# Turning rows with VectorE and small transfers instead of TensorE, and storing expert slots from GpSimd

## The chip, the cores and the metric

The kernel runs on one core of a Trainium2 chip. A core has five engines, each with its own in-order stream of instructions: TensorE (PE in the profile; its weight loads are PEld), VectorE (DVE), ScalarE (ACT), GpSimd (POOL) and SyncE (SP, which only starts transfers here). They meet through semaphores. The metric is the device time of one execution in microseconds (us); lower is better.

## What is computed

The reference is a stack of four layers on x (4 batches, 256 tokens, 256 features), float32 throughout. Each layer adds a cross attention to a context (4 x 512 x 128) and then a feed-forward, both on layer-normalised rows:

```
x = x + L0_xattn(layernorm(x), ctx)   # 16 heads of 16, normalised queries and keys, 16 extra context rows
x = x + L0_ffn(layernorm(x))          # best 4 of 64 "arrows" per token, low rank, plus a dense product
x = x + L1_xattn(layernorm(x), ctx)   # 16 heads of 128, 8 key/value heads
x = x + L1_ffn(layernorm(x))          # softmax router, best 2 of 8 experts, SwiGLU, plus a shared expert
x = x + L2_xattn(layernorm(x), ctx)   # as L1
x = x + L2_ffn(layernorm(x))          # each token to one of two experts
x = x + L3_xattn(layernorm(x), ctx)   # as L1
x = x + L3_ffn(layernorm(x))          # best 64 tokens of a batch through a wide feed-forward
```

## The kernel before

**Turned rows.** A matrix product contracts over partitions, so the rows that enter it must be stored with features on partitions. A batch's normalised rows xn lie with tokens on partitions, as [128, 2 halves, 256]; `layernorm_T` (L938 to L948) turns them into xnT by four TensorE transposes against an identity matrix into a PSUM bank, which ScalarE copies to SBUF. `context_T` (L906 to L911) does the same for a batch's context, four transposes and one copy, into cT. `turned1` (L2189 to L2196) stores the rows of layer 1's feed-forward to the DRAM buffer xd, from which tokens are later gathered by index, and turns them as well for the router.

**Order.** The large stages stand in a block in which the program's order is the order of TensorE, ScalarE, VectorE and GpSimd. SyncE is not in that list; the framework places its transfers itself.

**Layer 0's attention** walks through the batches b in eight half-steps i. `between(b, i)` (L1589 on) prepares batch n = b + 1: for n of 2 and 3, half-step 0 turned the context, copied its last rows (`last_context`, on GpSimd) and turned the normalised rows.

**Attentions 1 to 3** (`attention`, from L1795) walk through 32 units: a batch b and a pair of heads hp, 0 to 7. A unit makes the next unit's queries on TensorE (`queries`: seven block products and then sums on VectorE and ScalarE, `four`), then scores (L1923), exponentials on ScalarE (L1926) and the product with the context (L1931). GpSimd and VectorE add up the exponentials (`summed`) and divide. Beside this the next batch's rows are readied: in pair 1 the statistics (`Norm`), in pair 3 the normalised tokens, in pair 5 `layernorm_T`, in pair 6 `x_sums`, which adds blocks of the turned rows on VectorE for the seven-product scheme. The first batch of each attention is turned ahead of it. The callback `beside1` (L2248) does the router's work for batch b - 1 during attention 1: `Norm` in pair 3, tokens in pair 4, `turned1` in pair 5, `chosen` in pair 6, each at the end of its unit. Weights of the next feed-forward come on SyncE in batch 0, each behind the end of a unit (`load_waiting`).

**Layer 1's feed-forward** packs the chosen tokens into 20 slots (blocks) of 128. The loop over j (L2567 on) keeps several blocks going at once. Iteration j gathers block j+2 (`gather`, an indirect DMA by GpSimd, four buffers), transposes it on TensorE (`turn_in`), multiplies block j+1 with its expert's weights (`rise`), and block j with the second matrices (`fall`). At every odd j the pair (j-1, j) is finished by `last_rows` and `store`: ScalarE scales PSUM into yr, and a transfer on SyncE writes yr to the DRAM buffer yd. In the code, gather(j+2) and turn_in(j+2) stand first in an iteration, the stores last:

```
for j in range(-1, NBLK + 1):
    if j + 2 < NBLK:
        if j + 2 >= 4:
            blocks[j + 2].gather()
        ...
        blocks[j + 2].turn_in()
    ...
            for one in pair:
                one.store()
```

When all slots are stored, indirect DMAs by GpSimd (`Back`, L2505 on) fetch each token's two results from yd.

Of the kernel before, what the change touches and what calls it, by code (L numbers as in the profile page):

```python
# [9 lines left out]
F32 = mybir.dt.float32  # L10
# [7 lines left out]
P = 128  # L18
B, S, D = 4, 256, 256
NC = S // P  # L20
ND = D // P
# [815 lines left out]
def bounded_path(ctx: ExitStack, tc: tile.TileContext, t, out: bass.AP, over):  # L837
# [8 lines left out]
    first = ctx.enter_context(ExitStack())  # L846
    f0w = first.enter_context(tc.tile_pool(name="f0w", bufs=1, side="right"))
    w0 = first.enter_context(tc.tile_pool(name="w0", bufs=2, side="right"))
    ring = first.enter_context(ExitStack())
    ringo = ctx.enter_context(ExitStack())  # L850
    banks = {
# [99 lines left out]
        xn = Norm(b, name).tokens(keep)  # L951
        return xn, layernorm_T(xn, name)

    def normalised(name):

        after = layernorm(0, f"{name}_0")
        for b in range(B):
            _, xnT = after
            if b + 1 < B:
                after = layernorm(b + 1, f"{name}_{b + 1}")  # L960
            yield b, xnT

    raws = {}

# [68 lines left out]
    with tc.manual_schedule(engines={E.PE, E.Activation, E.DVE, E.Pool}):  # L1033
# [555 lines left out]
        def between(b, i):  # L1589

            n = b + 1
            if n == 1:
                if i == 0:
                    for k0 in range(0, NK, 2):
                        project_k(n, k0)()
                    scale[n] = Scale(n)
                    scale[n].square(False, NC, NQK)
                    xnTs[n] = layernorm_T(xns[n], f"a0_{n}")
                elif i == 1:
                    project_q(n)()  # L1600
                    scale[n].square(False, 0, NC)
                    project_v(n)
                elif i == 2:
                    scale[n].sum()
                    scale[n].power()
                elif i == 5:
                    transposed(n, 0)
                    transposed(n, 2)
                elif i == 6:
                    transposed(n, 4)  # L1610
            elif n < B:
                if i == 0:
                    context_T(n)
                    last_context(n)
                    xnTs[n] = layernorm_T(xns[n], f"a0_{n}")
                elif i == 1:
                    project_q(n)()
                elif i == 2:
                    for k0 in range(0, NK, 2):
                        project_k(n, k0)()  # L1620
                    scale[n] = Scale(n)
                    scale[n].square(False)
                elif i == 3:
                    project_v(n)
                    scale[n].sum()
                elif i == 4:
                    scale[n].power()
                elif i == 6:
                    transposed(n, 0)
                    transposed(n, 2)  # L1630
            if n + 1 < B:
                if i == (5 if n == 1 else 6):
                    norms[n + 1] = Norm(n + 1, f"a0_{n + 1}")
                elif i == (6 if n == 1 else 7):
                    xns[n + 1] = norms[n + 1].tokens()

            i0 = 4 if b == B - 1 else 6
            if b > 0 and i in (i0, i0 + 1):
                output0(b - 1, (i - i0,))
            if b == 1:  # L1640
                if i == 0:
                    bias_rows()
                elif i == 1:
                    bias_columns()
                elif i == 2:
                    output_bias()
            if b == B - 1:
                if i == 0:

                    mf = w0.tile([B * NK, P], F32, tag="hs", name="mf", bufs=1)  # L1650
                    nc.vector.tensor_copy(mf, m8)
                    xns["mf"] = mf
                elif i == 1:
                    pmk = bank("mm", [P, B * NK], "pmk")
                    nc.tensor.transpose(pmk, xns["mf"], ident[: B * NK, : B * NK])
                    nc.vector.tensor_scalar(
                        mbias.rearrange("p b k -> p (b k)"), pmk, 1.0, -NEG, ALU.subtract, ALU.mult
                    )
                elif i == 2:
                    score_bound()  # L1660
                elif i == 3:

                    nc.vector.tensor_reduce(
                        quad[:, :32], ident.rearrange("p (a q) -> p q a", q=32), AX.X, ALU.add
                    )
                    for j in range(1, 4):
                        nc.vector.tensor_copy(quad[:, 32 * j : 32 * (j + 1)], quad[:, :32])
            if b == B - 1:
                if i in (0, 2, 6):
                    norms["f", i // 2] = Norm(min(i // 2, 2), f"f0_{min(i // 2, 2)}")  # L1670
                if i in (1, 3, 7):
                    xns["f", i // 2] = norms["f", i // 2].tokens()
                if i in (3, 5):
                    k = (i - 3) // 2
                    xnTs["f", k] = layernorm_T(xns["f", k], f"f0_{k}")
                if i == 4:
                    arrows[0] = Arrows(0)
                    arrows[0].vectors()
                if i == 5:
                    arrows[0].routes()  # L1680
# [114 lines left out]
    def attention(L, m_sb, n_sb, first_xnT=None, after=None, at_end=None, chunk=None, within=None):  # L1795
# [11 lines left out]


        with tc.tile_pool(name=f"att{L}", bufs=2) as ap:
            xnTs, xns, xxs, norms, qTs, pqs, outs, sums = {}, {}, {}, {}, {}, {}, {}, {}  # L1810
            units = [(b, hp) for b in range(B) for hp in range(H // 2)]
            m_x = ap.tile([P, H // 2, 3, P], F32, tag="m_x", name=f"m_x{L}", bufs=1)
            n_x = ap.tile([P, H // 2, 3, P], F32, tag="n_x", name=f"n_x{L}", bufs=1)
# [220 lines left out]
            for n, (b, hp) in enumerate(units):  # L2034
                if b + 1 < B:
                    if hp == 1:
                        norms[b + 1] = Norm(b + 1, f"a{L}_{b + 1}")
                    elif hp == 3:
                        xns[b + 1] = norms[b + 1].tokens()
                if n == 0:  # L2040
                    first_queries(1)
                    x_sums(0)
                elif n + 1 < len(units):
                    queries(*units[n + 1])
                if b + 1 < B and hp == 5:
                    xnTs[b + 1] = layernorm_T(xns[b + 1], f"a{L}_{b + 1}")
                if b + 1 < B and hp == 6:
                    x_sums(b + 1)
                if b == 0:
                    m_sums((hp + 2) % (H // 2))  # L2050
                if n:
                    summed(*units[n - 1], *half)

                last, i = ((b, 0), hp - 4) if hp >= 4 else ((b - 1, 1), hp)
                prev = last[0] >= 0
                h0 = 4 * last[1]
                if prev and i >= 2:
                    for k in (2 * i - 4, 2 * i - 3):
                        o_sums(last[0], h0 + k, nc.gpsimd)
                half = heads(b, hp)  # L2060
                if prev and i == 0:
                    quotients(*last)
                if prev and i in (1, 2):
                    for k in (2 * i - 2, 2 * i - 1):
                        divided(last[0], h0 + k, nc.gpsimd)
                if b == 0 and hp < 6:
                    n_sums(hp)
                if (b, hp) == (1, 0):
                    n_sums(6)
                    n_sums(7)  # L2070
                if prev and i == 3:
                    out = Output(*last)
                    if last != (B - 1, 0):
                        out.products()
                        out.add()
                if after:
                    after(b, hp)
# [108 lines left out]
    nc.vector.memset(taken[:, 0, :], 0.0)  # L2186
    xnT1 = {}

    def turned1(b, xn):  # L2189
        nc.sync.dma_start(xd[b * S : (b + 1) * S, :].rearrange("(c p) d -> p c d", p=P), xn)  # L2190
        xnT1[b] = fx.tile([P, ND, S], F32, tag=f"xnT{b}", name=f"xnT_f1_{b}")
        pt = bank("t", [P, ND, S], f"pxn_f1_{b}")
        for c in range(NC):
            for d in range(ND):
                nc.tensor.transpose(pt[:, d, c * P : (c + 1) * P], xn[:, c, d * P : (d + 1) * P], ident)
        nc.scalar.copy(xnT1[b], pt)  # L2196
# [51 lines left out]
    def beside1(b, hp):  # L2248
        if b == 0:
            load_waiting(2)  # L2250
        if b > 0:
            if hp == 3:
                ahead1[b] = Norm(b - 1, f"f1_{b - 1}")
            elif hp == 4:
                ahead1[b] = ahead1[b].tokens()
            elif hp == 5:
                turned1(b - 1, ahead1[b])
            elif hp == 6:
                chosen(b - 1)

# [4 lines left out]
    with tc.manual_schedule(engines={E.PE, E.Activation, E.DVE, E.Pool}):  # L2265
        back = ExitStack()
        backp = back.enter_context(tc.tile_pool(name="back", bufs=4, side="right"))
        with tc.tile_pool(name="f1", bufs=2) as fp:
# [161 lines left out]
            class Block:  # L2430
# [66 lines left out]
                def store(self):  # L2497
# [2 lines left out]
                    done["slots"] = nc.scalar.activation(  # L2500
                        yr, self.py, AF.Copy, scale=state["wslot"][:, j : j + 1]
                    ).ins
                    nc.sync.dma_start(yd[j * P : (j + 1) * P, :], yr)

            class Back:  # L2505

# [947 lines left out]
```

## Time and profile before

| | us |
|---|---|
| median of 3 runs | 1388.01 |
| the runs | 1386.84 to 1388.09 |
| the profiled execution | 1386.64 |
| its span, first to last instruction | 1384.9 |
| TensorE busy | 1374.5 |
| VectorE busy | 887.1 |
| GpSimd busy | 683.9 |
| ScalarE busy | 580.2 |

The mean granted TensorE clock is 0.999 of full speed. A row of a timeline gives the start in us from the span's start, the busy time, the engine, the line of the code, the operation and its tiles; in brackets, the idle time before it and what ended that. Matmuls overlap in TensorE's pipeline, so their busy columns add up to more than the time that passes; starts are what counts. A float32 matmul is listed as two instructions, a transpose as one. The rows that give a stretch's busy time have its start and end, its length, busy us of TensorE, weight loads, VectorE, ScalarE and GpSimd with their numbers of instructions, the granted clock, the share of DMA and GB/s.

Where the stages lie in this execution: attention 1 from 217 to 541 us or so, the slots of layer 1's feed-forward from 575 to 628, attention 2 from 650 to 970, attention 3 from 1028 to 1352.

### The profile page before, as it was taken

How to read it: one execution, taken by the hardware profiler on the slowest of the kernel's cores; microseconds unless marked ns; L12 is line 12 of the kernel's file. 1: busy time of each engine (PE TensorE's matmuls, PEld its weight loads, DVE VectorE, ACT ScalarE, POOL GpSimd, SP SyncE). 2: the span in 40 equal slices, each digit the busy share in tenths (PEclk: the TensorE clock that was granted, in tenths of full speed). 3: DMA queues.
4: the chain of work that ended last, by engine and by line, in shares of the span. 5: the costliest groups of instructions: out<-in, count | busy, mean ns of one | idle time of the engine just before them, and what ended most of it. 6: DMA issues, size and time to landing. Idle time of an engine off the chain costs nothing.

```text
span 1384.9 us, 20011 instructions
## 1 busy us (share of the span) xinstructions
PE 1374.5 (99%) x7277; PEld 908.1 (66%) x7277; DVE 887.1 (64%) x2026; ACT 580.2 (42%) x1148; POOL 683.9 (49%) x829
## 2 busy tenths in 40 slices
PE   9999999999999999999999999999999999999998
PEld 7665676566656667887565666666975656666667
DVE  6667863665666547655666756558656758566676
ACT  5766454433343332356434333333364344333331
POOL 4223333566565445232577654556315675445561
PEclk9999999999999999999999999999999999999999
DMA  5000220300000001172110000000332000000001
GB/s 170 2 1 2 76 77 21 78 17 1 9 0 9 1 9 34 47 238 67 39 54 8 16 1 9 0 0 16 120 117 65 8 4 4 0 1 0 1 0 34
DMA packets 50849, 47.10 MB, mean 34 GB/s; under 512 B 8755, under 2 KB 46868, under 8 KB 50742
## 3 DMA queue, kind: packets, MB, share of 16 engines
q1 hardware_dynamic: 46406, 37.69, 8.9%
q0 software_dynamic: 2544, 6.95, 1.8%
q8 instruction: 60, 0.98, 0.3%
q10 hardware_dynamic: 1792, 1.10, 0.3%
q14 instruction: 47, 0.39, 0.1%
HBM read 38.78 MB, written 6.95 MB: 33 GB/s over the span
## 4 chain that ended last, share of the span: by engine, by line
PE 95%; POOL 2%; DVE 1%; DMA 1%; issue 0%; ACT 0%; ACTq 0%; SPq 0%; POOLq 0%; DVEq 0%
PE ps L1923 23%; PE po L1931 23%; PE paq L1893 6%; PE pao L1893 5%; PE pbq L1893 4%; PE pbo L1893 4%; PE ps L1378 3%; PE po L1388 2%; PE pyf L1512 2%; PE paf L1462 2%; PE pgu L2471 2%; PE psh L2292 2%; PE py L2017 2%; PE pn L1008 1%; PE pb L2876 1%; PE pm L992 1%
## 5 line engine op out<-in xcount | busy, mean ns | idle before, releaser
L1942 POOL TENSOR_TENSOR half<-pT 128x1024 f32<-128x1024 f32 x93 | 218.4, 2349 | 287.1 <-ACT pT L1926 214.8
L1923 PE MATMUL ps<-qT,cT 128*128 128x512 f32 x768 | 345.6, 593 | 0.0
L1931 PE MATMUL po<-pT,c_sb 128*128 128x512 f32 x768 | 345.3, 592 | 0.0
L1926 ACT ACTIVATE pT<-ps,mbias 128x512 f32<-128x512 f32 x384 | 263.8, 687 | 155.3 <-PE ps L1923 140.0
L1931 PEld LDWEIGHTS po<-pT,c_sb 128*128 128x128 f32 x768 | 145.8, 190 | 183.2 <-issue 183.2
L1923 PEld LDWEIGHTS ps<-qT,cT 128*128 128x128 f32 x768 | 138.9, 190 | 138.4 <-issue 136.3
L1935 ACT COPY oT<-po 128x512 f32<-128x512 f32 x96 | 56.2, 586 | 265.2 <-PE po L1931 265.2
L1978 POOL TENSOR_TENSOR oT<-oT,wide 128x512 f32<-128x512 f32 x84 | 106.8, 1292 | 0.0
L1903 DVE TENSOR_TENSOR qT<-qT,paq 128x128 f32<-128x128 f32 x90 | 25.5, 283 | 96.0 <-ACT qT L1902 96.0
L1382 ACT ACTIVATE pT<-ps 128x512 f32<-128x512 f32 x128 | 66.0, 602 | 25.8 <-PE ps L1378 25.6
L1950 DVE TENSOR_TENSOR half<-half 128x512 f32<-128x512 f32 x96 | 71.8, 748 | 2.7 <-POOL half L1940 2.5
L1952 DVE STREAM_TRANSPOSE turned<-half 128x512 f32<-128x512 f32 x96 | 68.3, 711 | 6.3
L1903 DVE TENSOR_TENSOR w<-w,pao 128x128 f32<-128x128 f32 x21 | 6.0, 286 | 103.0 <-ACT w L1902 103.0
L1893 PE MATMUL paq<-xnT_a,m_sb 128*128 128x128 f32 x360 | 71.4, 280 | 0.0
L1893 PE MATMUL paq<-xx,m_x 128*128 128x128 f32 x360 | 69.6, 275 | 0.0
L1893 PEld LDWEIGHTS paq<-xnT_a,m_sb 128*128 128x128 f32 x360 | 57.2, 192 | 16.7 <-issue 8.5
L1956 DVE TENSOR_REDUCE sums<-turned 128x16 f32<-128x512 f32 x96 | 65.9, 686 | 3.3
L1893 PE MATMUL pao<-n_x,ox 128*128 128x128 f32 x336 | 65.0, 275 | 0.0
L1902 ACT COPY qT<-paq 128x128 f32<-128x128 f32 x90 | 23.9, 265 | 94.1 <-PE paq L1893 94.1
L1906 DVE TENSOR_TENSOR qT<-qT,pbq 128x384 f32<-128x384 f32 x90 | 49.9, 554 | 9.7 <-DVE qT L1905 0.5
L1893 PEld LDWEIGHTS paq<-xx,m_x 128*128 128x128 f32 x360 | 54.7, 192 | 0.0
L1977 DVE STREAM_TRANSPOSE wide<-rz 128x512 f32<-128x512 f32 x84 | 54.4, 686 | 0.0
(490 smaller groups left out, 2547.3 us busy)
## 6 DMA issues: line engine op xcount, KB each, us to landing
wq<-in_L_wqT SPq DMA_DIRECT2D x11, 512.0 KB, 4.2
wo<-in_L_wo SPq DMA_DIRECT2D x11, 512.0 KB, 5.1
yd<-yr SPq DMA_DIRECT2D x20, 128.0 KB, 3.6
xd<-xn_f SPq DMA_DIRECT2D x8, 256.0 KB, 2.3
w<-in_F_w SPq DMA_DIRECT2D x4, 512.0 KB, 3.3
wk<-in_L_wkT SPq DMA_DIRECT2D x11, 128.0 KB, 4.0
wv<-in_L_wvT SPq DMA_DIRECT2D x11, 128.0 KB, 4.4
yd<-yb SPq DMA_DIRECT2D x9, 128.0 KB, 2.4
```

What stands on the lines that cost most here:

```text
L1382: nc.scalar.activation(pT[kp][:, j], ps[j], AF.Exp)
L1893: nc.tensor.matmul(p[:, at, :], lhsT=lhsT, rhs=rhs, start=(k == 0 and at == 0), stop=(k == len(of) - 1 and i == which[-1]),)
L1923: nc.tensor.matmul(ps, lhsT=cT[:, b, k * P : (k + 1) * P], rhs=qT, start=True, stop=True)
L1926: nc.scalar.activation(pT[:, k, :], ps, AF.Exp, bias=mbias[:, b, k : k + 1])
L1931: nc.tensor.matmul(po, lhsT=c_sb[:, b, k, :], rhs=pT[:, k], start=(k == 0), stop=(k == NK - 1))
L1935: done["head"] = nc.scalar.copy(raw, po).ins
L1942: nc.gpsimd.tensor_tensor(half, pT[:, 0:2], pT[:, 2:4], ALU.add)
L1950: nc.vector.tensor_tensor(part, half[:, 0], half[:, 1], ALU.add)
L1952: nc.vector.transpose(turned.rearrange("p f i -> p (f i)"), part)
L1956: nc.vector.tensor_reduce(sums[b, hp // 4][:, hp % 4, :], turned, AX.X, ALU.add)
L1977: nc.vector.transpose(wide, rzs[b, hp // 4][:, hp % 4, :, None].to_broadcast([P, NB, 32]))
L1978: eng.tensor_tensor(outs[b, hp], outs[b, hp], wide.rearrange("p f i -> p (f i)"), ALU.mult)
```

## The change

Nine turns in attentions 1 to 3 (batches 1 to 3), three of layer 1's router rows (batches 0 to 2) and two contexts in layer 0 (batches 2 and 3) are no longer TensorE's. VectorE transposes their 32 x 32 squares into a buffer y, and 16 transfers on SyncE, of 32 partitions each in runs of 128 bytes, carry the squares to their partitions of xnT or cT. In attentions this starts in pair 3 with the tokens instead of pair 5; the router's starts at the end of pair 4 instead of 5; a context starts in half-step 2 of the batch before, so six half-steps ahead of its use. The buffer y is a new pool in layer 0, and otherwise takes turns with xn in a tag of two buffers. The slots' stores are started by GpSimd instead of SyncE, at the same place of the code.

```
+    early = first.enter_context(tc.tile_pool(name="early", bufs=1, side="right"))
...
+    def squares(shape, name, soon):
+        return early.tile(shape, F32, tag="y", name=name) if soon else lnp.tile(shape, F32, tag="xn", name=name)
+
+    def turned_aside(dst, src, name):
+
+        y = squares([P, 4, 4, 32], f"y_{name}", True)
+        nc.vector.transpose(
+            y.rearrange("p q n s -> p n q s"), src.rearrange("p (n q s) -> p n q s", q=4, s=32)
+        )
+        to = dst.rearrange("p (n i s) -> p i n s", i=4, s=32)
+        for i in range(4):
+            for q in range(4):
+                nc.sync.dma_start(to[32 * q : 32 * q + 32, i], y[32 * i : 32 * i + 32, q])
+
+    def layernorm_aside(xn, name, xnT, soon=False):
+
+        y = squares([P, 4, ND, NC, 32], f"y_{name}", soon)
+        for c in range(NC):
+            nc.vector.transpose(
+                y[:, :, :, c].rearrange("p q d s -> p d q s"), xn[:, c, :].rearrange("p (d q s) -> p d q s", d=ND, s=32)
+            )
+        to = xnT.rearrange("p d (c i s) -> p i d c s", c=NC, s=32)
+        for i in range(4):
+            for q in range(4):
+                nc.sync.dma_start(to[32 * q : 32 * q + 32, i], y[32 * i : 32 * i + 32, q])
+        return xnT
+
+    def rows_tile(name):
+        return lnp.tile([P, ND, S], F32, tag="xnT", name=f"xnT_{name}")
...
             elif n < B:
                 if i == 0:
-                    context_T(n)
                     last_context(n)
                     xnTs[n] = layernorm_T(xns[n], f"a0_{n}")
...
             if n + 1 < B:
+                if i == 2:
+                    turned_aside(cT[:, n + 1, :], c_sb[:, n + 1].rearrange("p k c -> p (k c)"), f"c{n + 1}")
...
                     elif hp == 3:
-                        xns[b + 1] = norms[b + 1].tokens()
+                        name = f"a{L}_{b + 1}"
+                        xnTs[b + 1] = layernorm_aside(norms[b + 1].tokens(), name, rows_tile(name))
...
-                if b + 1 < B and hp == 5:
-                    xnTs[b + 1] = layernorm_T(xns[b + 1], f"a{L}_{b + 1}")
...
-    def turned1(b, xn):
+    def turned1(b, xn, aside=False):
         nc.sync.dma_start(xd[b * S : (b + 1) * S, :].rearrange("(c p) d -> p c d", p=P), xn)
         xnT1[b] = fx.tile([P, ND, S], F32, tag=f"xnT{b}", name=f"xnT_f1_{b}")
+        if aside:
+            layernorm_aside(xn, f"f1_{b}", xnT1[b])
+            return
...
             elif hp == 4:
-                ahead1[b] = ahead1[b].tokens()
-            elif hp == 5:
-                turned1(b - 1, ahead1[b])
+                turned1(b - 1, ahead1[b].tokens(), True)
...
-                    nc.sync.dma_start(yd[j * P : (j + 1) * P, :], yr)
+                    nc.gpsimd.dma_start(yd[j * P : (j + 1) * P, :], yr)
```

An unused generator, normalised, goes as well.

More of the change, by code (lines that the diff above doesn't have):

```diff
@@ L952, in layernorm @@
         return xn, layernorm_T(xn, name)
[L954 to L961, printed above, removed]
+    def squares(shape, name, soon):
[22 more added lines that the diff above has]
+        return lnp.tile([P, ND, S], F32, tag="xnT", name=f"xnT_{name}")
     raws = {}
@@ L1809, in attention @@
         with tc.tile_pool(name=f"att{L}", bufs=2) as ap:
-            xnTs, xns, xxs, norms, qTs, pqs, outs, sums = {}, {}, {}, {}, {}, {}, {}, {}
+            xnTs, xxs, norms, qTs, pqs, outs, sums = {}, {}, {}, {}, {}, {}, {}
             units = [(b, hp) for b in range(B) for hp in range(H // 2)]
```

## The prediction, made before the changed kernel was run

> **What bounds the kernel now.** I read part 1 of the page first, the summary and the chain next, then the timeline of the stage in which the slots are stored.
>
> ```profile
> span 1384.9 us, 20011 instructions
> PE 1374.5 (99%) x7277; PEld 908.1 (66%) x7277; DVE 887.1 (64%) x2026; ACT 580.2 (42%) x1148; POOL 683.9 (49%) x829
> ...
> PE 95%; POOL 2%; DVE 1%; DMA 1%; issue 0%; ACT 0%; ACTq 0%; SPq 0%; POOLq 0%; DVEq 0%
> ```
>
> TensorE is the bound in nearly every stage. So a matmul taken out is worth its issue time, and anything new that TensorE waits for is paid in full. Everything else has room: VectorE is idle 36% of the span.
>
> TensorE in the unit (batch 0, heads pair 5) of attention 1, with a layernorm's four transposes:
>
> ```profile
> 266.45 0.39 PE L1893 MATMUL pbq<-xx,m_sb 128*128 128x128 f32 x2
> 266.68 0.60 PE L944 MATMUL pxn_a<-ident,xn_a 128*128 128x128 f32 x4
> 267.11 1.45 PE L1923 MATMUL ps<-qT,cT 128*128 128x512 f32 x3
> ```
>
> Busy columns overlap; what counts is start to start: 267.11 - 266.68 = 0.43 us for a group of four.
>
> The stage of the 20 slots in layer 1's feed-forward, TensorE and then GpSimd:
>
> ```profile
> 591.12 0.60 PE L2489 MATMUL pyr<-wd,gT 128*128 x2
> 591.64 0.48 PE L2495 MATMUL pyr<-wd,gR 48*128 x1
> ...
> 592.28 0.44 PE L2446 MATMUL pxg<-ident,xg 128*128 128x128 f32 x2
> 592.55 1.49 PE L2471 MATMUL pgu<-xgT,we 128*128 128x128 f32 x12
> ```
>
> ```profile
> 583.49 0.94 POOL L2438 DMA_INDIRECT xg<-xd,who  x1 [0.60 <-PE pxg L2446]
> 585.47 0.95 POOL L2438 DMA_INDIRECT xg<-xd,who  x1 [1.04 <-PE pxg L2446]
> ...
> 638.06 0.94 POOL L2512 DMA_INDIRECT yg<-yd,where  x1 [23.16 <-DMA yd<-yr]
> 639.31 0.95 POOL L2512 DMA_INDIRECT yg<-yd,where  x1 [0.30 <-DVE taken L2692]
> ```
>
> The transposes at 592.28 are block 6's turn_in (the seventh such group from 579.77 on). Block 6's gather is the issue at 583.49, 8.8 us ahead: GpSimd waits only for a free buffer. The last pair of rows shows that a DMA's wait stands in GpSimd's own queue: 23.16 us in front of one gather, nothing passing it inside the stage. ScalarE's rows of the slots, which the moved stores wait for:
>
> ```profile
> 592.38 0.84 ACT L2500 ACTIVATE yr<-pyr,wslot 128x256 f32<-128x256 f32 x2 [0.46 <-PE pyr L2495]
> ```
>
> **The transposes taken off TensorE.** Nine groups of four go from attentions 1 to 3 and three from layer 1's router rows (start to start 354.81 to 355.25 there): 12 x 0.435 = 5.2 us. Two contexts in layer 0 go (48.76 and 80.69). The second is followed by 0.34 us of TensorE idle at 81.69, until VectorE's y_sb, so a gain may turn into that wait; the next tile also takes an earlier bank of the ring, which may free more. Between 0 and 0.8 us each, I take 0.4: 0.8. Sum 6.0 us. ScalarE loses 14 evictions of 0.59 us, off the path.
>
> **What replaces them.** VectorE gets two transposes of 256 elements a row per norm. The nearest row is the 512-element STREAM_TRANSPOSE of L1952, 711 ns; half of it or all of it bounds one, so 0.7 to 1.4 us a norm, and I take 0.9 (a fixed part remains). They stand in front of the query sums (four) of the next unit, and behind them the summed of the last one. TensorE wants those sums one unit later: the sums at 406.49 to 408.2, already behind 3.68 us of token scaling, serve scores of the following unit, about 7 us on. Cover 7 us against 0.9: nothing. Without it, 12 x 0.9 = 11 us. The two 0.71 us ones of the contexts lie in layer 0, where VectorE is busy 65.28 of 93 us: nothing.
>
> SyncE issues 16 transfers per turned tile, 14 tiles. The nearest row is the eight pieces of wo, 16 rows and 32 KB each (x8 in 4.22 us from 11.64): 0.53 us each, landing 2.9 us after. Sixteen take 8.5 + 2.9 = 11.4 us, from half (0.3 us each) to twice. An attention's rows start in pair 3 and are wanted by x_sums in pair 6, at least 3 x 8.4 = 25 us; the router's start at the end of pair 4 and are wanted at the end of pair 6, 17 us; contexts have six half-steps of about 4 us, 24 us. The store of xd ahead of the router's and the weight loads in batch 0 are passed on the same queue: one more issue (0.34 us), or one unit of waiting for a head, still inside 25. The buffer y (shared with xn) comes round after about 17 us, again more than 11.4. I take 0 for all of it. If a turn were late, VectorE's x_sums would wait, and with it the sums behind it, then TensorE.
>
> **The stores on GpSimd.** This is the costly edit. In the code a pair of stores comes at the end of each odd iteration j, and the next iteration starts with gather(j+3) and at once turn_in(j+3) on TensorE. Now store(j-1) and store(j) wait on GpSimd for ScalarE's yr; behind them queue gather(j+3) and gather(j+4). Their lead of 8.8 us is gone, and the one who waits is TensorE's turn_in, with all its matmuls behind. It happens for blocks 4, 6, ... 18: eight times. An odd block's gather lands 1.25 us after the even one's (639.31 - 638.06), while its turn_in comes 2.0 us later (594.32 - 592.28): no stall.
>
> One stall, from the time TensorE is ready (592.28 in this pair):
> - first yr done and seen: SyncE started its store at 592.88, +0.60
> - two stores on GpSimd. No plain DMA of GpSimd is in the trace. Below, SyncE's price for this store, 0.34 us (they then wait for the second yr, ending +0.94); above, 1.31, the longest indirect one. I take the usual indirect one, 0.95 with 0.30 between, since it is the same queue and 128 rows: 2.5
> - the gather lands 2.85 us after its start (639.31 to the add that waited, 642.16); bounds 2.7 and 3.2
> Sum 0.60 + 2.50 + 2.85 = 5.95, say 6.0 us; bounds 4.1 (1.0 + 0.35 + 2.7) and 7.0. Times eight: 48 us, 33 to 56.
>
> **The clock after a stall.** At the end of the run TensorE issues nothing after 1379.7:
>
> ```profile
> 1380.00:1382.00 2.00, 0.00 (x0) 0.00 (x0) 0.67 (x3) 0.00 (x0) 0.00 (x0) 1.00 0.46 127
> 1382.00:1383.00 1.00, 0.00 (x0) 0.00 (x0) 0.00 (x0) 0.00 (x0) 0.00 (x0) 0.66 0.47 136
> 1383.00:1384.00 1.00, 0.00 (x0) 0.00 (x0) 0.00 (x0) 0.00 (x0) 0.00 (x0) 0.50 0.11 25
> ```
>
> 0.66 in one slice and 0.50 in the next put the drop at 1382.3, 2.6 us after the last matmul. How long it stays down is seen at the start: 18 warming matmuls in 4.01 us (1.52 to 5.53), 223 ns each, where such matmuls take 111 later; the rate changes near 6.6, so 5.1 us at half rate, 2.55 us lost. [...] I take the trace's 20. [...]
>
> [...] The row: SyncE's stores x6 spread over 12.02 us without TensorE waiting. [...]
>
> **The stage's end.** Before, the last store was sent at 633.47, landed at 637.12, and the first gather of results started at 638.06. Two stores of 0.95 + 0.30 from 633.1 start the second at 634.35 and land it near 637.2: 0, from -0.5 to +1.5.
>
> **Sum.** -6.0 + 48 + 20 + 0 = +62 us. Against the profiled execution, 1386.64 us (span 1384.9 and 1.7 around it): 1448.6. That execution lies 1.4 under the median of the runs, 1388.01; so 1450.
>
> **The rivals.**
> - Cheap stores, warm clock: the low bounds. 1388 - 6 + 33 = 1415, up to 1430 with half of the drops. For it: SyncE's 0.34 us. Against: every GpSimd DMA in the trace takes 0.94 or more.
> - Faster: the gathers keep their lead, because stores do not hold what is queued behind them. Place: GpSimd's queue in the slots' stage; price 0; it decides once an even gather starts at least 2.85 us before its turn_in. Then only the 6 us remain: 1382. For it: SyncE's stores cost nothing; the turned rows all have 11.4 us against 17 or more. Against: the 23.16 us row, and that in this block GpSimd kept the code's order elsewhere (the gather at 647.37 came behind the norm's power at 646.46, though its buffers were free).
> - Turned rows late: beyond (17 - 2.9) / 16 = 0.9 us a transfer the router's product waits, beyond 1.4 an attention's x_sums. At 2 us each, 35 against 25: 10 us on nine tiles, 90 us, so about 1540 with the stalls.
> - The change not doing what it says: if turning merely moved TensorE's wait (as at 81.69), 1388 + 68 = 1456; inside the range.
>
> **Chances.** Stalls with the cold clock 0.60 (1450); cheap stores 0.20 (1415 to 1430); the gathers keep their lead 0.15 (1382); late rows 0.05. About 0.2% (2.8 us) is what a measurement of this kernel can tell from no change. The faster case leaves 1382 with a spread of 3, so faster 0.14, same 0.02, slower 0.84. The range takes in the first two cases: from 1412, the cheap end less a measurement's 3 us, to 1388 - 6 + 56 + 38 = 1476, where both upper bounds meet. It leaves out 0.2.
>
> **What would show it.** Right: in the slots' stage GpSimd's even gathers start behind two DMA rows of yd<-yr, TensorE idles about 6 us before every second pxg with the gather as releaser, and the granted clock there falls well under 1; the stage grows from 53 us to about 120. Attention 1 shrinks by 2.6 us (six groups), attentions 2 and 3 by 1.3 each, and no x_sums waits for a DMA. Wrong: gathers still 5 us or more ahead of their turn_in (the second rival), plain stores far under 0.9 us (the first), or waits for xnT in pair 6 (the third).

## The result and the profile after

The changed kernel takes 1454.2 us (median of 5 runs, 1454.12 to 1455.6), the kernel before 1387.64 in the same rounds: a ratio of 1.0485, interval 1.0469 to 1.05. It is slower by 66.6 us; 62 were predicted. The profiled execution took 1454.12 us.

The summary and the chain of its page:

```profile
span 1452.4 us, 20237 instructions
PE 1386.3 (95%) x7221; PEld 918.6 (63%) x7221; DVE 897.7 (62%) x2052; ACT 573.4 (39%) x1134; POOL 696.4 (48%) x849
...
PEclk9999999999999999867999999999999999999999
...
PE 89%; issue 5%; POOL 2%; DVE 1%; DMA 1%; ACT 0%; ACTq 0%; DVEq 0%; POOLq 0%
```

TensorE issues 56 matmuls fewer and still is busy 11.8 us longer: in one place, slices 17 to 19 of 40, its clock drops to 0.8, 0.6 and 0.7, and the same work takes longer there. TensorE's share of the chain falls from 95 to 89%; "issue", time that no instruction explains, rises from 0 to 5%. The waits of TensorE say who is behind it (total, times, longest):

```profile
PE pxg L2469 <- DMA xg<-xd,who: 54.2, 8, 8.4
```

Eight waits for gathers, 54.2 us, in the slots' stage. GpSimd in that stage:

```profile
586.56 1.16 POOL L2526 DMA_DIRECT2D yd<-yr  x2 [11.42 <-ACT yr L2523]
588.02 1.01 POOL L2461 DMA_INDIRECT xg<-xd,who  x1 [0.30 <-issue]
589.34 0.98 POOL L2461 DMA_INDIRECT xg<-xd,who  x1 [0.30 <-issue]
602.30 1.16 POOL L2526 DMA_DIRECT2D yd<-yr  x2 [11.99 <-ACT yr L2523]
603.76 1.01 POOL L2461 DMA_INDIRECT xg<-xd,who  x1 [0.30 <-issue]
```

And TensorE's first matmul after each wait:

```profile
594.03 0.66 PE L2469 MATMUL pxg<-ident,xg 128*128 128x128 f32 x2 [8.27 <-DMA xg<-xd,who]
...
606.70 0.66 PE L2469 MATMUL pxg<-ident,xg 128*128 128x128 f32 x2 [5.20 <-DMA xg<-xd,who]
...
621.33 0.66 PE L2469 MATMUL pxg<-ident,xg 128*128 128x128 f32 x2 [8.33 <-DMA xg<-xd,who]
```

GpSimd stands for the rows of the slots (yr), 11.4 and 12.0 us here and 7.7 to 12.1 later, issues two stores, and only then the gather that TensorE is waiting for. The lead of 8.8 us has become a delay. The waits come in two lengths, four of about 8.35 us and four of 5.2. The short one is 0.80 from TensorE ready (601.50) to the first store, 1.46 to the gather's start and 2.94 to its use. In the long one the gather takes 588.02 to 594.03, 6.01 us. SyncE's timeline shows what goes on then, the first of four weight transfers of layer 2, 1.25 MB together:

```profile
586.65 0.37 SPq L998 DMA_DIRECT2D n_sb<-in_L_wqT  x1
587.07 0.50 SPq L998 DMA_DIRECT2D m_sb<-in_L_wkT  x1
```

They are sent when the second yr of a pair is done, behind blocks 1, 5, 9 and 13, so beside every second stalled gather. The stretches of two stalls and the work behind each (start and end, length, busy us of PE, PEld, DVE, ACT and POOL, clock, share of DMA, GB/s):

```profile
586.60:594.00 7.40, 0.00 (x0) 0.00 (x1) 0.00 (x0) 0.03 (x1) 3.11 (x4) 0.69 0.76 247
594.00:601.50 7.50, 7.47 (x36) 6.47 (x36) 1.76 (x6) 1.84 (x6) 0.00 (x0) 0.63 0.00 1
601.50:606.70 5.20, 0.00 (x1) 0.03 (x1) 0.77 (x2) 0.84 (x2) 3.14 (x4) 0.98 0.23 76
606.70:613.00 6.30, 6.30 (x36) 5.47 (x36) 1.77 (x6) 1.84 (x6) 0.00 (x0) 0.75 0.07 23
```

The long stall moves 247 GB/s, the short one 76. Behind each, TensorE works through the two blocks of a pair. In the kernel before, a pair took 4.75 us from transpose to transpose (592.28, shown above, to 597.02), at a clock of 1.00:

```profile
597.02 0.44 PE L2446 MATMUL pxg<-ident,xg 128*128 128x128 f32 x2
```

```profile
587.50:622.50 35.00, 34.79 (x265) 29.18 (x264) 18.89 (x51) 19.15 (x59) 11.47 (x12) 1.00 0.77 232
```

Now it takes 7.5 and 6.3 us at clocks of 0.63 and 0.75: 2.7 and 1.55 us lost.

The whole difference between the two profiled executions, stage by stage from the first matmuls of each:

| | us |
|---|---|
| layer 0, to attention 1's first queries | -1.15 |
| attention 1, to its last product | -2.37 |
| from there to the first slot's transpose | +1.7 |
| slots to attention 2's first queries (70.4 to 140.6) | +70.2 |
| attention 2 and 3 | -1.29 each |
| behind the last matmul | +1.7 |
| sum | +67.5 = 1452.4 - 1384.9 |

Of the +70.2, 54.2 are waits. The other 16.0 are what is left, and the clock accounts for them: added up pair by pair, the losses behind the eight waits make 16.9 us, and the rest of the stage is 0.9 shorter.

### The profile page after: what moved, and what is told of

The parts are those of the page before. It is cut to its first block, busy times and chain, and to the rows that moved or that the text cites. A ratio compares the mean times of both kernels' runs of the same rounds, so it can differ in the third digit from the quotient of the medians.

```text
span 1452.4 us, 20237 instructions
## 1 busy us (share of the span) xinstructions
PE 1386.3 (95%) x7221; PEld 918.6 (63%) x7221; DVE 897.7 (62%) x2052; ACT 573.4 (39%) x1134; POOL 696.4 (48%) x849
## 4 chain that ended last, share of the span: by engine, by line
PE 89%; issue 5%; POOL 2%; DVE 1%; DMA 1%; ACT 0%; ACTq 0%; DVEq 0%; POOLq 0%
PE ps L1946 22%; PE po L1954 22%; PE paq L1916 6%; PE pao L1916 5%; PE pbq L1916 4%; PE pbo L1916 4%; PE ps L1400 3%; PE po L1410 2%; PE pyf L1534 2%; PE paf L1484 2%; PE psh L2315 1%; PE py L2040 1%; PE pm L1014 1%; PE pn L1030 1%; PE pb L2899 1%
## 5 line engine op out<-in xcount | busy, mean ns | idle before, releaser
L1979 DVE TENSOR_REDUCE sums<-turned 128x16 f32<-128x512 f32 x96 | 65.8, 686 | 3.3
L2505 DVE TENSOR_TENSOR gT<-sg,pgu 128x128 f32<-128x128 f32 x20 | 5.8, 288 | 92.3 <-ACT sg L2500 92.3
L2469 PE MATMUL pxg<-ident,xg 128*128 128x128 f32 x40 | 10.9, 366 | 54.2 <-DMA xg<-xd,who 54.2
L2526 POOL DMA_DIRECT2D yd<-yr x20 | 11.5, 578 | 95.9 <-ACT yr L2523 95.9
```

The lines of the kernel that those rows point to most:

```text
L1979: nc.vector.tensor_reduce(sums[b, hp // 4][:, hp % 4, :], turned, AX.X, ALU.add)
```

## Experiments

The theory: the turns gain about 6 us, and the stores cost all of the rest, because the gathers queue behind them on GpSimd. The rivals: part of the loss is the turns'; GpSimd's stores are slow in themselves; the waits are harmless without the clock.

**One part alone.** The changed kernel with the stores back on SyncE:

```
-                    nc.gpsimd.dma_start(yd[j * P : (j + 1) * P, :], yr)
+                    nc.sync.dma_start(yd[j * P : (j + 1) * P, :], yr)
```

> The changed kernel with the slots' stores back on SyncE; the turned rows stay on VectorE and transfers. Theory (the loss is all in the slots' stage, the turns are a gain): 6 us under the kernel before, 1381.5, at most 1385 if the tail (+1.7) and the one clock drop in the token lists (+1.7) of the changed kernel belong to the turns; no wait of TensorE for xg. Rival (the 224 new transfers also cost, on SyncE's queue or by late rows): 1388 or more.

It took 1380.59 us (1379.66 to 1381.63) against 1387.13, ratio 0.9951, interval 0.9936 to 0.9966. The opposite, the kernel before with only its stores moved to GpSimd (the same line, the other way):

> The kernel before with only the slots' stores moved to GpSimd. Theory: the stage loses 54 us of waits and 16 of clock as in the changed kernel, with none of the 6 gained: 1458, from 1455 to 1461. Rival (the stores cost only together with the new transfers): under 1400.

It took 1459.5 us (1458.4 to 1460.92), ratio 1.0517, interval 1.0499 to 1.0536, with the same waits:

```profile
PE pxg L2446 <- DMA xg<-xd,who: 54.1, 8, 8.4
```

The parts add up: -6.5 and +72.4 make +65.8 of the +66.6 measured. So the turns are a gain, and the stores alone lose.

**Order or price.** If the place in GpSimd's queue is the cause, gathers written ahead of the stores must end it with the stores still on GpSimd. First five blocks ahead:

```
+                if j + 5 < NBLK:
+                    blocks[j + 5].gather()
                 if j + 2 < NBLK:
-                    if j + 2 >= 4:
-                        blocks[j + 2].gather()
```

> The changed kernel, stores still by GpSimd, but each gather written three iterations earlier (block j+5 in iteration j), so that no store of a later pair stands in front of it. Same transfers, same engine, other order. Theory (it is the order in GpSimd's queue): no wait for xg, 1381.5, up to 1386 with the tail and the clock drop. Rival (a store by GpSimd is dear by itself: its issue, its descriptors or its landing): over 1400.

It took 1388.91 us (1387.53 to 1390.47), ratio 1.0011, interval 1.0002 to 1.002: about 65 us are gone, but it stays 8 above the turns alone and above the 1386 that I had allowed. Its trace shows four waits left, 7.1 us in all, for blocks 7, 11, 15 and 19. Their sum, and the first of them:

```profile
PE pxg L2469 <- DMA xg<-xd,who: 7.1, 4, 2.4
```

```profile
592.50 0.41 PE L2469 MATMUL pxg<-ident,xg 128*128 128x128 f32 x2 [1.44 <-DMA xg<-xd,who]
```

Its gather started at 586.45, among the four weight transfers (sent from 585.07 to 587.06), and took 6.05 us to its use: the slow landing again. TensorE wanted it at 591.06, so its lead was only 4.6 us, because it still stood behind a pair of stores (584.98). So I wrote each gather as soon as its buffer has been read, which is nearly an iteration earlier (not two, as the expectation has it) and puts gather 7 ahead of that pair:

```
                     blocks[j + 2].turn_in()
+                    if j + 6 < NBLK:
+                        blocks[j + 6].gather()
```

with gather(4) behind turn_in(0).

> The changed kernel, stores still on GpSimd, but each gather is written as soon as its buffer is read: gather(j+6) right behind turn_in(j+2), gather(4) behind turn_in(0), so that it stands two iterations further ahead in GpSimd's queue than with the gathers written five ahead. Theory (order alone makes the stall; what remained there, 7.1 us in four waits, was gathers that had some 5 us of lead and took longer beside the weights of layer 2): a lead near 9 us again, no wait of TensorE for a gather, clock 1.00 in the stage; 1380.6 of the turns alone plus the 1.8 us by which all kernels with stores on GpSimd ended later after their last matmul: 1382.4 (1380.5 to 1384). Rival (stores on GpSimd cost something of themselves, as GpSimd still stops for each pair's yr): some of the 7.1 us stays, 1385 to 1389.

It took 1381.7 us (1381.1 to 1384.65), ratio 0.9958, interval 0.9944 to 0.9973. No wait for a gather is left. GpSimd now, and TensorE's transposes of blocks 8 and 9:

```profile
584.94 1.16 POOL L2526 DMA_DIRECT2D yd<-yr  x2 [1.98 <-ACT yr L2523]
586.40 1.01 POOL L2461 DMA_INDIRECT xg<-xd,who  x1 [0.30 <-issue]
587.72 1.23 POOL L2461 DMA_INDIRECT xg<-xd,who  x1 [0.30 <-issue]
```

```profile
594.03 0.44 PE L2469 MATMUL pxg<-ident,xg 128*128 128x128 f32 x2
596.07 0.38 PE L2469 MATMUL pxg<-ident,xg 128*128 128x128 f32 x2
```

The stores take what they took in the changed kernel and this pair waits 1.98 us for its rows, but the gathers behind it are wanted only at 594.03, 7.6 us on. From the first slot's transpose to attention 2's queries it is 69.9 us, against 69.4 with the turns alone and 140.6 in the changed kernel. So the stores on GpSimd cost the stage about half a microsecond; their place ahead of a gather that is wanted at once cost 70.

**The clock.** The changed kernel with matmuls of the identity, whose results nobody reads, in front of the even transposes; 36 or 22 of them fill each wait:

```
+                    if j + 2 >= 4 and j % 2 == 0:
+                        pw = bank("o", [P, P], f"pfill{j}")
+                        for _ in range(36 if j % 4 == 2 else 22):
+                            nc.tensor.matmul(pw, lhsT=ident, rhs=ident, start=True, stop=True)
```

> The changed kernel with idle matmuls in front of the even blocks' turn_in: 22 (4.9 us at full rate) where the wait was 5.2 us, 36 (8.0 us) where it was 8.3. They fill the waits and change nothing else. Theory (16 us of the loss are the clock halving after each wait): 1454 - 16 = 1438, down to 1435, granted clock near 1 in the stage. Rival (TensorE is slow after a wait for another reason, or the clock falls anyway): 1454 or more by the filling.

It took 1436.43 us (1436.32 to 1437.89), ratio 1.0354, interval 1.0336 to 1.0371, with a clock of 1.00 in the stage, where the changed kernel had 0.75 (the changed kernel second):

```profile
586.60:660.00 73.40, 72.81 (x603) 67.31 (x603) 15.56 (x43) 16.47 (x50) 21.96 (x28) 1.00 0.33 106
```

```profile
586.60:695.80 109.20, 55.80 (x296) 48.69 (x296) 19.72 (x55) 21.40 (x65) 25.14 (x33) 0.75 0.27 87
```

The delays are still there, 54.6 us in all from the first filling matmul to the transpose; TensorE is merely not idle in them. 17.8 us are gone by the medians, and the stage is 16.7 shorter in the profiled executions: that is what the cold clock costs.

**The long waits.** The weights of layer 2 sent one iteration later, behind the copy that follows a transpose (ScalarE's `xgT`), when the stalled gather has landed:

```
-                if j in (5, 9, 13):
-                    load_raw(2, j // 4, done["slots"])
+                if j in (6, 10, 14):
+                    load_raw(2, j // 4, done["turned"])
```

and the first at j = 2 in the same way.

> The changed kernel with the four sets of layer 2's raw weights (1.25 MB each) sent after the stalled turn_in (behind its copy xgT, one iteration later) instead of behind the pair's last yr, where they share the DMA engines with the awaited gather. Theory (the gather beside a load lands in 6.0 us instead of 2.9): the four waits of 8.3 us become 5.2, 12 us less, and each clock loss behind them shrinks from 2.65 to 1.55 us, 4 us less: 1438, from 1436 to 1442. Rival (every second gather lands late for another reason, such as the stores ahead of it in the ring): 1454.

It took 1442.81 us (1442.05 to 1444.77), ratio 1.0395, interval 1.0377 to 1.0413, just above the range I gave. All eight waits are now 5.1 to 6.0 us, 11.5 less in all than 54.2, so the transfers did make the long ones:

```profile
PE pxg L2469 <- DMA xg<-xd,who: 42.7, 8, 6.0
```

The clock did not follow. From one transpose behind a wait to the next it takes 11.3 to 12.8 us; less the 4.75 of work and the wait, 1.4 to 3.0 us are lost, 2.1 on average, as much as the 2.7 and 1.55 of the changed kernel. I had expected 1.55 for all. Waits of nearly one length lose from 1.4 to 3.0 us; what decides between them was not tested.

**How much cover the turns need.** In the kernel with the turns alone I made an attention's tokens and turn later than pair 3, so that less stands ahead of x_sums (pair 6):

```
-                    elif hp == 3:
+                    elif hp == 6:
                         name = f"a{L}_{b + 1}"
                         xnTs[b + 1] = layernorm_aside(norms[b + 1].tokens(), name, rows_tile(name))
```

> The kernel with the turns alone (stores on SyncE, 1380.6), but the tokens and the turn of an attention's next batch are made in pair 6 instead of pair 3, just ahead of the sums of turned rows that need them. Theory (a turn costs nothing only because it has 25 us of lead; it takes 0.8 us of VectorE, then 16 issues of 0.6 and 1.8 to landing, 11.4 us): VectorE stands about 10 us at x_sums, with the query sums of the unit after next behind it, which TensorE wants some 6 us later: a wait of TensorE of 3 to 8 us for each of nine batches, and up to 2.5 us of clock each; 1410 to 1470, about 1430. Rival (the sums have slack for all of it): 1381 to 1384.

It took 1476.28 us (1474.05 to 1478.72), ratio 1.063, interval 1.0611 to 1.0648. From the waits of VectorE and of TensorE:

```profile
DVE xx L1847 <- DMA xnT_a<-y_a: 93.0, 9, 11.2
```

```profile
PE paq L1916 <- DMA xnT_a<-y_a: 62.9, 9, 10.1
```

VectorE stands 10.3 us for each of nine batches, as the working of a turn has it, and TensorE 7.0. Some 5 us of smaller waits come on top. The other 29 us of the 97 in the span come with a mean clock of 0.968 against 0.998 and were not taken apart. The waits are in the range I gave, the total is just above it, with more lost beside the waits than the 2.5 us each that I allowed. The same in pair 5:

> As the kernel with the turn in pair 6, but tokens and turn in pair 5. By the same working the rows land about 1.6 us after x_sums would start, less than VectorE's idle time of a unit (2 to 3.6 us), so TensorE should not notice: 1380.6, 1379.5 to 1382. If the turn took clearly over 11.4 us, or VectorE had no slack, 1390 or more.

This expectation failed: 1431.14 us (1429.24 to 1431.21), ratio 1.0307, interval 1.0291 to 1.0322. VectorE's waits:

```profile
DVE xx L1847 <- DMA xnT_a<-y_a: 38.8, 9, 6.5
...
DVE y_a L973 <- DMA xnT_f<-y_f: 19.0, 2, 9.5
```

The rows come 2.8 to 6.5 us after x_sums could start, not 1.6. In attention 1 the turn of the router's rows, started at the end of pair 4, also holds the buffer y: twice VectorE stands 9.5 us, and TensorE 7.3 behind it. In the first batch a delay of 2.8 us reached no matmul; delays of 4.0 to 5.2 in attention 2 cost TensorE 2.2 to 4.5 us. In attention 3 two delays of 3.1 us cost nothing, and one of 2.9 stood ahead of a wait of 4.8 for another of VectorE's tiles. So the sums have between 0.8 us of slack (5.2 late, 4.5 lost) and some 3, and two pairs later is already too late. Not all of the 50 us come of the shorter lead: 14.6 us of TensorE's waits are the two behind the shared buffer y. That the turns are free is a matter of where they start.

## Why the prediction came out right

**The direction and the mechanism** were right. The even gathers start behind two rows of yd<-yr, TensorE waits eight times, for those blocks and no others, and the clock falls behind the waits, to 0.63 and 0.75 in the two pairs shown. The second rival, gathers that keep their lead (1382), is what the kernel with early gathers does, and it needs another order of the code. Cheap stores with a warm clock (1415 to 1430) is half true: a store takes 0.58 us, well under the 0.9 that I had named as the sign of this rival, yet a stall still took 5.2 us and the clock was not warm. The rival "the change does not do what it says" gave 1456, nearer to the result than my 1450, and is refuted all the same: the turns alone gain 6.5 us. A total can agree for the wrong reason. Mine had luck too: in the profiled execution the waits were 6.2 us more than I took, the clock's loss 4.0 less, and 3.4 us I had not foreseen.

**Transposes taken off, -6.0.** Measured -6.1 (1.15 + 2.37 + 1.29 + 1.29). Attention 1 gave 2.37 of 2.6, layer 0 1.15 instead of 0.8; no wait at 81.69 took it back.

**What replaces them, 0.** Right. One turn in the kernel with the turns alone, SyncE's and VectorE's rows:

```profile
323.59 10.27 SPq L979 DMA_DIRECT2D xnT_a<-y_a  x16
```

```profile
322.77 0.76 DVE L973 STREAM_TRANSPOSE y_a<-xn_a 128x256 f32<-128x256 f32 x2
```

Two transposes take 0.76 us, under the 0.9 assumed; sixteen issues take 10.3 us and a piece lands in 1.8 (median), about 11.5 to 12 in all. I had 11.4, by two errors that cancel: 8.5 for the issues and 2.9 for the landing. No x_sums waits for it. The 7 us of cover that I gave VectorE in pair 3 were not measured: in the kernel with the turns alone no matmul waits for the sums behind these transposes, so 0 was right, and in pair 5 the slack was only 0.8 to 3 us.

**One stall, 0.60 + 2.50 + 2.85 = 5.95.** Measured 0.80 + 1.46 + 2.94 = 5.20 in the short ones: the term of the two stores was too large. I took an indirect gather's 0.95 and a gap of 0.30 for each; a plain store takes 0.58, two follow each other with no gap, and one gap of 0.30 stands behind both. In the long ones the term of the landing was too small, 6.01 for 2.85, because I did not look at what SyncE sends at that moment, although its load stands in the code right behind the stores. The trace before would have told me: it has landings of 2.7 to 6.0 us for gathers into xg, and I bounded the term by 2.7 and 3.2. The errors have opposite signs: 6.8 us on average, 54.2 for 48.

**The clock, 20.** Measured 16.0 as the rest of the stage (16.9 pair by pair) and 17.8 by filled waits, so 2.0 to 2.2 us a stall where I took 2.5. I took one number from the run's start, eight times; single stalls lost from 1.4 to 3.0, in the changed kernel 1.4 to 1.6 behind the short ones and 2.7 behind the long ones. The range has 0 and 38 us for this term at its two ends, and no run shows either for stalls of this length: eight of 5.2 to 8.4 us cost the 16 to 18 above, and waits of 2.4 us at most, with the gathers five blocks ahead, left the clock at 1.00 in the stage.

**The end of the stage, 0.** From the end of the last pair of transposed blocks to attention 2's first queries it took 24.2 us before (625.98 to 650.18) and 23.6 after (694.91 to 718.54), so nothing was lost there.

**Not foreseen: +3.4 us.** The end: from VectorE's last instruction to the end of the span it is 4.2 to 4.4 us in the four profiled executions with stores on SyncE, and 5.9 to 6.2 in the six with stores on GpSimd. So some 1.7 us go with the move, though the last of these stores lies some 750 us earlier (702.8 in the changed kernel); what happens in them was not found. The other 1.7 us are the clock in the stretch of the token lists. The changed kernel first, the kernel before second:

```profile
569.00:572.30 3.30, 3.30 (x9) 2.59 (x9) 1.83 (x10) 0.00 (x0) 1.84 (x2) 0.50 0.07 19
```

```profile
572.30:575.70 3.40, 3.40 (x18) 2.89 (x18) 2.39 (x11) 0.00 (x0) 1.72 (x2) 1.00 0.05 10
```

TensorE is busy throughout, at half the rate, right behind 32 matmuls of only 40 columns. This is not the change: of ten profiled executions, one of each kernel, seven show it, that of the stores alone (without the turns) among them, and three do not: the kernel before and the two with the gathers written earlier, which have the turns. It lies ahead of the first store. Why it comes in some executions is open.

## What to carry to other kernels

The moved stores stood in GpSimd's order here: it waited up to 12.1 us for their rows, with the gathers queued behind. Before moving a transfer to another engine, list what is queued behind it and how soon that is wanted, for the price of the issue itself (0.58 us here) was the smallest part. If it must move, move the instructions that are wanted early ahead of it; the same stores cost the stage 70 us or about half a microsecond. And ask of every new wait which transfers run in the same microseconds (a gather took 2.94 us to its use, and 6.01 beside the weights), and of every transfer taken as free how much lead it has: three pairs, by my estimate 25 us, hid a turn completely, and two pairs less, with a clash over the buffer y, cost 50 us.

## What the runs showed of the hardware that I had not expected

- A gather of 128 rows took 2.94 us from its start to its use without a weight load beside it, and 6.0 beside weights of 1.25 MB.
- A plain store on GpSimd, 0.58 us, is cheaper than an indirect gather (0.95 to 1.0 in most cases), and two follow each other without the gap of 0.30 us; on SyncE it was 0.34.
- The granted clock fell to 0.50 for 3.3 us with TensorE busy 3.30 of 3.30 (the changed kernel, 569.00 to 572.30); of ten profiled executions seven show such a drop ahead of the stores.
- Kernels with these stores on GpSimd ended some 1.7 us later after their last work: 5.9 to 6.2 us after VectorE's last instruction, where it was 4.2 to 4.4 with the stores on SyncE.
